# Wide layers as seven products of quarters instead of eight, with sums of weights formed on chip

## The chip, the cores and the metric

One core of one Trainium2 chip runs the whole kernel in one launch. The metric is the time of that launch on the device, in microseconds (us), lower is better. Engines are named as in the profile: PE is TensorE (PEld its weight loads), DVE is VectorE, ACT is ScalarE, POOL is GpSimd, SP is SyncE, which here only issues DMAs. SBUF is the on-chip memory that all engines read; PSUM holds the results of matmuls, in eight banks of 128 x 512 floats.

## The reference

A sequence of 4 x 1024 tokens with 256 channels passes a feed-forward network, a state-space mixing layer, and the same feed-forward network again.

```python
def ffn(x, w1_w, w1_s, w2_w, w2_s, h1_w, h1_s, h2_w, h2_s, w3_w, w3_s):
    lin = lambda x, w, s: einsum("bsi,oi->bso", x, w) * s      # w is ternary: -1, 0 or 1
    h = silu(lin(x, w1_w, w1_s)) * lin(x, w2_w, w2_s)          # 256 -> 1024
    h = gelu(lin(h, h1_w, h1_s))                               # 1024 -> 1024, exact gelu
    h = gelu(lin(h, h2_w, h2_s))                               # 1024 -> 1024
    return lin(h, w3_w, w3_s)                                  # 1024 -> 256

def mixing(x, ...):            # state-space layer: a long convolution over the sequence
    K = s4d_kernel(...)        # 256 channels x 1024 taps
    y = irfft(rfft(x, n=2048) * rfft(K, n=2048))[:1024]
    return gelu(y) @ W.T + b

x = x + 0.5 * ffn(layernorm(x))       # x: [4, 1024, 256] float32
x = x + mixing(layernorm(x))
x = x + 0.5 * ffn(layernorm(x))
```

The two layers `h1` and `h2`, 1024 to 1024, are the wide layers. They hold most of the arithmetic.

## The kernel before

**Tiles and blocks.** The 4096 tokens are cut in blocks of 512. Eight blocks, f0 to f7, go through the first feed-forward network, and eight, g0 to g7, through the second. Tokens lie along the free dimension, 512 to a tile, and channels along the 128 partitions. A block passes through four stages in `ffn`: the gate stage (eight pairs of tiles `pa` and `pb`, 8 matmuls to a pair, silu on ACT at L362 and the product on DVE at L363), the two wide layers (tiles `p`, gelu on ACT at L377), and the last stage (tiles `po`, in `last_squares`, or in `last_tokens` for the block that ends the kernel).

**Two parts.** The matmuls run in the fp32r format, in which a general float32 value is not held exactly. The weights, being -1, 0 or 1, are. An activation is therefore carried in two parts: the high part is a cast on ACT (L367 and L379), the low part is the difference between the value and its cast, a subtraction of two SBUF tiles on DVE (`low_part`, L287). `linear` (L344) multiplies each weight tile with both parts into one PSUM bank. A tile of a wide layer is 8 input chunks x 2 parts = 16 matmuls, 128 x 128 weights by 512 columns, so a layer is 128 of them and the two layers 256. All weights stay in SBUF (`h1_sb` and `h2_sb` take 32 KB a partition each); POOL's DMA queue brings them at the start.

**Mixing layer.** The convolution is done with discrete Fourier transforms as matmuls, and with products and sums of spectra on DVE. This work, `all_aside`, is a generator that is cut in small steps. Between two tiles of a wide layer `ffn` calls `tick()`, which advances it until work worth `STEP_WORK` = 2500 units (130 an operation plus its columns) has been issued, or until it reports a pause, and `ahead()`, which advances the preparation of the next block (load, layer norm, transposition of 32 x 32 squares with a pass through DRAM). Where the mixing layer has nothing to do, `tick()` runs `weight_checks`, which reads all weights again and compares them with the copies in fp32r; if one differed, a second version of the whole would run in float32. The mixing of a sequence starts once both of its blocks have left the first network (f1 for the first sequence), and must be done before its first block in the second one is prepared.

**Order.** Each engine executes its own instructions in a fixed order, made from the order of the calls in the source by a scheduler. The DMAs of SP and those of POOL form two queues. A tile of the pools `half` (19 buffers of 2 KB a partition), `ring` (15, for the two-part activations) or `psum` (8 banks, shared by everything) waits until the last reader of the buffer that it reuses is done. The output additions `y` of a block are on POOL (L406), with the stores issued by POOL (L408).

Of the kernel before, what the change touches and what calls it, by code (L numbers as in the profile page):

```python
# [31 lines left out]
JQ = J // 2  # L32
N_WARM = 9


STEP_WORK, OP_WORK, MIN_WORK = 2500, 130, 300
PAUSE = "pause"
N_CHECKS = 44

# [58 lines left out]
def macaron_layers(  # L98
# [22 lines left out]

    nc = tc.nc
# [7 lines left out]
    psum = ctx.enter_context(tc.tile_pool(name="psum", bufs=8, space=bass.MemoryType.PSUM))  # L130

    work_done = 0
# [16 lines left out]
    def bank(name):  # L149
        return psum.tile([P, 512], F32, tag="ps", name=name)  # L150

    def half(name, *shape, dtype=F32):

        return work.tile([P, *(shape or (512,))], dtype, tag="half", name=name, bufs=19)

    def ring(name, *shape, dtype=F32):

        return work.tile([P, *shape], dtype, tag="ring", name=name, bufs=15)
# [9 lines left out]
    h1_sb = keep.tile([P, KH, HID], wide, name="h1_sb")  # L168
    h2_sb = keep.tile([P, KH, HID], wide, name="h2_sb")
# [12 lines left out]
    k_hat = dram.tile([2 + len(PAIRS), 2, P, 2, D], F32, name="k_hat")  # L182

# [37 lines left out]


# [21 lines left out]
    for t, src in ((h1_sb, h1), (h2_sb, h2)):  # L244
        for k in range(0, KH, 2):
            weights_from.dma_start(t[:, k : k + 2, :], rows(src)[:, k : k + 2, :])
# [38 lines left out]
    def low_part(t, src):  # L285

        return nc.vector.tensor_tensor(t[:, 1, :], src, t[:, 0, :].bitcast(F32), ALU.subtract)  # L287

    def transposed(xn, name):


        pts = [bank(f"pt_{name}_{k}") for k in range(DC)]
# [59 lines left out]
    def ffn(xt, src, dst, blk, name, tick, ahead, final):  # L352


        ha = []
        for m in range(KH):
            pa, pb = bank(f"pa_{name}_{m}"), bank(f"pb_{name}_{m}")
            linear(pa, w1_sb, m, xt)
            linear(pb, w2_sb, m, xt)
            g = half(f"g_{name}_{m}")  # L360
            t = ring(f"ha_{name}_{m}", parts, TB, dtype=wide)
            nc.scalar.activation(g, pa, AF.Silu, scale=sc_sb[:, 0, m : m + 1])  # L362
            nc.vector.scalar_tensor_tensor(  # L363
                g if split else t[:, 0, :], pb, sc_sb[:, 1, m : m + 1], g, ALU.mult, ALU.mult
            )
            if split:
                nc.scalar.copy(t[:, 0, :], g)  # L367
                low_part(t, g)
            ha.append(t)
        for layer, w in ((2, h1_sb), (3, h2_sb)):  # L370
            hb = []
            for m in range(KH):
                ps = bank(f"p{layer}_{name}_{m}")
                linear(ps, w, m, ha)
                t = ring(f"h{layer}_{name}_{m}", parts, TB, dtype=wide)
                g = half(f"g{layer}_{name}_{m}") if split else t[:, 0, :]
                nc.scalar.activation(g, ps, AF.Gelu, scale=sc_sb[:, layer, m : m + 1])  # L377
                if split:
                    nc.scalar.copy(t[:, 0, :], g)  # L379
                    low_part(t, g)  # L380
                hb.append(t)
                ahead()
                if layer == 2 or m < KH - 1:
                    tick()
            ha = hb
        ahead(last=True)
        if name == "f0":
            nc.scalar.mul(w3s_half, w3s_half, 0.5)
        (last_tokens if final else last_squares)(ha, src, dst, blk, name)

    def last_squares(ha, src, dst, blk, name):
# [8 lines left out]
        for k in range(DC):  # L400
            ps = bank(f"po_{name}_{k}")
            linear(ps, w3_sb, k, ha)
# [7 lines left out]
    def last_tokens(ha, src, dst, blk, name):  # L410

        rest = []
        for i in range(0, JT, 2):
            xr = half(f"xr_{name}_{i}", 2, D)
            nc.sync.dma_start(xr, tokens(src, blk, i, 2))
            rest.append(xr)

        def result(ps, i, n):

            for e in range(n):  # L420
                for k in range(KH):
                    for part in range(parts):
                        nc.tensor.matmul(  # L423
                            ps[:, e * D : (e + 1) * D],
                            ha[k][:, part, (i + e) * P : (i + e + 1) * P],
# [16 lines left out]

        y = half(f"y_{name}_0", 2, D)
        ps = bank(f"po_{name}_0")
        result(ps, 0, 2)
        finish(ps, y, rest[0], 0, 2, nc.gpsimd)
        y = half(f"y_{name}_2", 2, D)
        for e in range(2):
            ps = bank(f"po_{name}_{2 + e}")
            result(ps, 2 + e, 1)  # L450
            finish(
                ps[:, 0:D], y[:, e : e + 1, :], rest[1][:, e : e + 1, :], 2 + e, 1, nc.vector
            )

    def weight_checks():

        todo = []
        for src, held in ((w1, w1_sb), (w2, w2_sb), (h1, h1_sb), (h2, h2_sb), (w3, w3_sb)):
            n_k, width = held.shape[1], held.shape[2]
            by = max(1, 512 // width)  # L460
            for k in range(0, n_k, by):
                for c in range(0, width, 512):
                    cols = slice(c, min(c + 512, width))
                    todo.append((rows(src)[:, k : k + by, cols], held[:, k : k + by, cols]))
        assert len(todo) == N_CHECKS

        def load(n):
            given = half(f"given_{n}", *todo[n][1].shape[1:])
# [5 lines left out]
        for n, (src, held) in enumerate(todo):  # L474
            given = following
            if n + 1 < len(todo):
                following = load(n + 1)
            stt(
                given,
                given,  # L480
                0.0,
                held.bitcast(F32),
                ALU.add,
                ALU.not_equal,
                accum_out=miss[:, n : n + 1],
            )
            yield

# [3 lines left out]
        nc.vector.tensor_reduce(total, miss[:, 0:N_CHECKS], axis=mybir.AxisListType.X, op=ALU.add)  # L492
        yield
        ps = psum.tile([1, 1], F32, tag="ps", name="p_bad")
# [109 lines left out]
    def kernel_steps():  # L604
# [7 lines left out]
        for g0 in range(0, DD, group):  # L612
# [34 lines left out]
            def products(d1, a):  # L647
# [3 lines left out]
                if at == 0:  # L651
                    pk = psum.tile([P, per_tile, 2, NB], F32, tag="ps", name=f"pk_{g0 + d1}")
# [46 lines left out]
    def spectrum(rows_of, name, over=1):  # L699
# [22 lines left out]
        def products(q, m):  # L722
            ps = []
            for e in range(2):
                ps.append(psum.tile([P, 2, D], F32, tag="ps", name=f"pf_{name}_{q}_{e}"))
# [17 lines left out]
        for n in (0, 2):  # L743
            qs = order[n : n + 2]
            if n == 0:
                for q, m in zip(qs, ms):
                    products(q, m)
                ms = [matrix(q) for q in order[2:4]]
                yield PAUSE
            for q in qs:  # L750
                sums(q)
            if n == 0:
                for q, m in zip(order[2:4], ms):
                    products(q, m)
            s, t = (u[q] for q in qs)
            halves.append((add(s, t, ALU.add, f"s{n}"), add(s, t, ALU.subtract, f"d{n}")))
            yield PAUSE if n == 0 else None
# [49 lines left out]
    def mix(b, xn):  # L807
# [92 lines left out]
        banks = [[bank(f"pi_{b}_{dc}_{e}") for e in range(2)] for dc in range(DC)]  # L900
        for q, m in enumerate(matrices):
            for e in range(2):
                for dc in range(DC):
                    for part in range(2):
                        nc.tensor.matmul(  # L905
                            banks[dc][e][:, q * P : (q + 1) * P],
# [5 lines left out]
        yts = [[half(f"yt_{b}_{dc}_{e}") for e in range(2)] for dc in range(DC)]  # L912
        for e in range(2):
            for dc in range(DC):
                nc.scalar.activation(yts[dc][e], banks[dc][e], AF.Gelu)
# [38 lines left out]
    done = []  # L954
# [52 lines left out]
    def tick():  # L1007

        nonlocal ticks, allowed, work_done
        ticks += 1  # L1010
        allowed = min(allowed, work_done) + STEP_WORK
        while work_done < allowed:
            at = work_done
            if next(aside, PAUSE) is PAUSE:
                if len(done) > 8 and allowed - work_done > OP_WORK + TB:
# [6 lines left out]
    warm = bank("warm")  # L1022
# [99 lines left out]
```

## Time and profile before

The three runs took 1405.35, 1405.5 and 1405.73 us: a median of 1405.5. The profiled execution took 1405.23 us in all, of which the profile's span is 1403.3 us. TensorE's granted clock was 0.999 over it. Shares are of the span; a group's mean is that of one instruction.

| what | busy or mean | count |
|---|---|---|
| matmuls of wide layers, start of one to start of the next | 226.6 ns | 4096 |
| weight loads (PEld) | 1161.4 us, 83% | 6492 |
| low parts (DVE, L287, 128x512) | 690 ns | 256 in wide layers |
| gelu (ACT, L377, 128x512) | 689 ns | 256 |
| casts (ACT, L379) | 619 ns | 256 |
| ACT table loads (L377) | 1283 ns | 51 |
| gate product (DVE, L363, one operand in PSUM) | 749 ns | 128 |
| additions on POOL (L406, 128x512) | 1.30 us | 30 |
| DMA traffic | 101.27 MB, mean 72 GB/s | |

The busy times of TensorE and of the other engines, and the chain of waits, are shown in the prediction. A duration in a group is how long one instruction took, its own start-up included, and dense instructions of one engine overlap a little. For matmuls the spacing of starts is the figure that adds up to time, since they are pipelined.

### The profile page before, as it was taken

What the parts mean: (1) busy time and instruction counts of PE and PEld (TensorE: products, weight loads), DVE (VectorE), ACT (ScalarE), POOL (GpSimd) and SP (SyncE); (2) the same over time, 40 slices, a digit from 0 to 9 for tenths busy, and PEclk for the clock granted to TensorE, in tenths of its full rate; (3) what the DMA queues carried; (4) which work ended last, traced back from release to release, by engine and by line L of the source; (5) the groups of instructions that cost most, each with busy time, mean ns of one, the idle gap of its engine ahead of it and who ended that gap; (6) DMA issues with size and microseconds to landing.
All of it is one profiled execution on the core that took longest, in us unless ns stands there. A gap on an engine that the chain in (4) does not pass through costs nothing.

```text
span 1403.3 us, 17882 instructions
## 1 busy us (share of the span) xinstructions
PE 1393.0 (99%) x6492; PEld 1161.4 (83%) x6492; DVE 838.6 (60%) x1614; ACT 707.6 (50%) x1070; POOL 266.3 (19%) x398
## 2 busy tenths in 40 slices
PE   8999999999999999999999999999999999999998
PEld 7888888888888888888888888888888888888887
DVE  6896567755547774387773568753566762542412
ACT  5986579644546344354352454533545342553532
POOL 4321012211312120320113201213112121121200
PEclk9999999999999999999999999999999999999999
DMA  9410101112231322422213404132223122511000
GB/s 355 117 20 26 35 16 46 30 48 77 67 96 30 113 71 73 136 60 84 61 53 113 113 31 138 20 97 74 86 70 82 43 63 98 135 22 39 15 16 19
DMA packets 111139, 101.27 MB, mean 72 GB/s; under 512 B 72304, under 2 KB 82544, under 8 KB 111040
## 3 DMA queue, kind: packets, MB, share of 16 engines
q1 hardware_dynamic: 93248, 55.37, 14.6%
q0 software_dynamic: 17520, 44.39, 11.1%
q8 instruction: 53, 0.87, 0.3%
q14 instruction: 46, 0.38, 0.1%
q10 hardware_dynamic: 272, 0.26, 0.1%
HBM read 76.91 MB, written 23.07 MB: 71 GB/s over the span
## 4 chain that ended last, share of the span: by engine, by line
PE 99%; DMA 1%; POOL 0%; DVE 0%; issue 0%; POOLq 0%
PE p_f L344 33%; PE p_g L344 33%; PE po_f L344 4%; PE pa_g L344 4%; PE pb_g L344 4%; PE pa_f L344 4%; PE pb_f L344 4%; PE po_g L344 4%; PE pi L905 2%; PE pf_m L727 2%; PE pw L930 2%; PE pk L654 1%; PE po_g L423 1%; DMA w_sb<-in_w_dram 1%; PE pf_k L727 0%; POOL w_sb L238 0%
## 5 line engine op out<-in xcount | busy, mean ns | idle before, releaser
L287 DVE TENSOR_TENSOR h_g<-g_g,h_g 128x512 fp32r<-128x512 f32 x128 | 88.6, 692 | 249.6 <-ACT h_g L379 249.3
L344 PE MATMUL p_f<-h_f,h_sb 128*128 128x512 f32 x1024 | 237.1, 391 | 0.0
L344 PE MATMUL p_g<-ha_g,h_sb 128*128 128x512 f32 x1024 | 236.2, 390 | 0.0
L344 PE MATMUL p_f<-ha_f,h_sb 128*128 128x512 f32 x1024 | 235.3, 390 | 0.0
L344 PE MATMUL p_g<-h_g,h_sb 128*128 128x512 f32 x1024 | 235.2, 390 | 0.0
L377 ACT ACTIVATE g_g<-p_g,sc_sb 128x512 f32<-128x512 f32 x128 | 88.2, 689 | 278.9 <-PE p_g L344 276.5
L344 PEld LDWEIGHTS p_g<-ha_g,h_sb 128*128 128x128 f32 x1024 | 192.1, 188 | 39.8
L344 PEld LDWEIGHTS p_g<-h_g,h_sb 128*128 128x128 f32 x1024 | 192.1, 188 | 39.8
L344 PEld LDWEIGHTS p_f<-h_f,h_sb 128*128 128x128 f32 x1024 | 191.8, 188 | 40.1 <-DVE h_f L287 0.3
L344 PEld LDWEIGHTS p_f<-ha_f,h_sb 128*128 128x128 f32 x1024 | 191.9, 188 | 39.8
L377 ACT ACTIVATE g_f<-p_f,sc_sb 128x512 f32<-128x512 f32 x128 | 87.7, 689 | 190.0 <-PE p_f L344 189.6
L287 DVE TENSOR_TENSOR h_f<-g_f,h_f 128x512 fp32r<-128x512 f32 x128 | 87.8, 690 | 149.0 <-ACT h_f L379 148.5
L317 POOL DMA_DIRECT2D moved<-sq_g x64 | 34.9, 552 | 330.3 <-DVE sq_g L140 290.7
L379 ACT CAST h_g<-g_g 128x512 fp32r<-128x512 f32 x128 | 79.3, 620 | 4.0
L379 ACT CAST h_f<-g_f 128x512 fp32r<-128x512 f32 x128 | 78.3, 618 | 2.9
L377 ACT ACT_TABLE_LOAD x51 | 65.4, 1283 | 26.0 <-PE p_f L344 14.3
L344 PE MATMUL pa_f<-xt_f,w_sb 128*128 128x512 f32 x256 | 69.0, 390 | 1.1 <-DVE xt_f L299 0.7
L344 PE MATMUL pb_f<-xt_f,w_sb 128*128 128x512 f32 x256 | 68.8, 389 | 0.0
L344 PE MATMUL pa_g<-xt_g,w_sb 128*128 128x512 f32 x256 | 68.4, 389 | 0.0
L344 PE MATMUL pb_g<-xt_g,w_sb 128*128 128x512 f32 x256 | 68.4, 389 | 0.0
L363 DVE SCALAR_TENSOR_TENSOR g_g<-pb_g,sc_sb,g_g 128x512 f32<-128x512 f32 x64 | 47.9, 749 | 31.5 <-PE pb_g L344 19.7
L317 POOL DMA_DIRECT2D moved<-sq_f x56 | 30.8, 556 | 181.2 <-DVE sq_f L140 181.2
(234 smaller groups left out, 1844.4 us busy)
## 6 DMA issues: line engine op xcount, KB each, us to landing
h_sb<-in_h_dram POOLq DMA_DIRECT2D x8, 1024.0 KB, 15.0
given<-in_h_dram SPq DMA_DIRECT2D x32, 256.0 KB, 3.6
kr<-k_hat SPq DMA_DIRECT2D x20, 256.0 KB, 2.6
ki<-k_hat SPq DMA_DIRECT2D x20, 256.0 KB, 2.8
xr_f<-in_x_dram SPq DMA_DIRECT2D x64, 64.0 KB, 2.4
x<-y_f POOLq DMA_DIRECT2D x64, 64.0 KB, 2.2
xm<-x SPq DMA_DIRECT2D x8, 512.0 KB, 3.7
m_m<-in_cosm_dram SPq DMA_DIRECT2D x16, 256.0 KB, 5.2
```

Source lines behind the costliest of these rows:

```text
L287: return nc.vector.tensor_tensor(t[:, 1, :], src, t[:, 0, :].bitcast(F32), ALU.subtract)
L317: stores.dma_start(moved[k].rearrange("(c r) a q -> a r c q", r=SQ)[a], sq[a * SQ : (a + 1) * SQ].rearrange("r c j s -> r c (j s)"),)
L344: nc.tensor.matmul(ps, w[:, k, m * P : (m + 1) * P], acts[k][:, part, :], start=(k == 0 and part == 0), stop=(k == n - 1 and part == parts ...
L363: nc.vector.scalar_tensor_tensor(g if split else t[:, 0, :], pb, sc_sb[:, 1, m : m + 1], g, ALU.mult, ALU.mult)
L377: nc.scalar.activation(g, ps, AF.Gelu, scale=sc_sb[:, layer, m : m + 1])
L379: nc.scalar.copy(t[:, 0, :], g)
L423: nc.tensor.matmul(ps[:, e * D : (e + 1) * D], ha[k][:, part, (i + e) * P : (i + e + 1) * P], w3_sb[:, k, :], start=(k == 0 and part == 0) ...
L654: nc.tensor.matmul(pk[0:NA, at + i, :, :].rearrange("p h b -> p (h b)"), a[:, i].rearrange("p a b -> p (a b)"), qd[d1 // per_tile][:, at + ...
L727: nc.tensor.matmul(ps[e][:, part, :], m[:, e, part, :], rows_of(q + JQ * e), start=True, stop=True)
L905: nc.tensor.matmul(banks[dc][e][:, q * P : (q + 1) * P], vs[q + JQ * e][:, part, dc * P : (dc + 1) * P], m[:, e, part, :], start=(part == ...
L930: nc.tensor.matmul(ps[:, e * D : (e + 1) * D], yts[dc][j // JQ][:, (j % JQ + e) * P : (j % JQ + e + 1) * P], wt_sb[:, dc, :], start=(dc == 0),
```

## The change

A wide layer is Y = A B with A the 1024 x 1024 weights and B the 1024 x 512 activations. Cut both in quarters: A11, A12, A21, A22 of 512 x 512, and B11, B12, B21, B22 of 512 inputs by 256 tokens. Multiplied plainly that is eight products. Winograd's form of Strassen's scheme needs seven:

- weights: S1 = A21 + A22, S2 = S1 - A11, S3 = A11 - A21, S4 = A12 - S2. These are small whole numbers.
- activations: T1 = B12 - B11, T2 = B22 - T1, T3 = B22 - B12, T4 = T2 - B21.
- products: A11 B11, S1 T1, S2 T2, A12 B21, S3 T3, S4 B22 and -A22 T4, with sums between them, some in PSUM by accumulation in the same bank, and three by a copy to SBUF and an addition.

The new function `winograd` writes the seven out in this order. One product is 4 output tiles x 4 input chunks x 2 parts = 32 matmuls of 256 columns. The differences T are formed on POOL (`less`), cast and split as before (`operand`; the low parts of B21 and B22 on POOL, the others on DVE), the intermediate products are copied by ACT (`kept`) and added by DVE (`plus`), and gelu works on pieces of 256 columns (`activated`). Block f0 uses `quartered`, eight products of quarters. Its ticks also run `weight_sums`, which loads the weights in pieces, forms the sums on DVE, ACT and POOL and stores them in DRAM, in `quarters`. From f1 on each product loads its weights, 1 MB, from there into one of four buffers (`slot`), three products ahead, through SP's queue. `h1_sb` and `h2_sb` are gone.

The eight banks of PSUM become six for the feed-forward network and two for the rest. There are fourteen ticks to a layer in place of eight, with `STEP_WORK` 1340. The checks of h1 and h2 no longer compare with copies in SBUF but test whether each weight is -1, 0 or 1, with two DVE operations for one piece in place of one, and begin when f4 is done. The last stage works on one half of the tokens after the other. The spectrum and the inverse transform are put in an order that needs two banks at a time. The core of the diff:

```diff
+QT = TB // 2          # 256 tokens
+QK = KH // 2          # 4 chunks of 128 inputs
+QW = HID // 2         # 512 outputs
+A11, S1, A12, S2, S3, S4, MINUS_A22 = range(7)
+ORDER = (A11, S1, S2, A12, S3, S4, MINUS_A22)
-STEP_WORK = 2500
+STEP_WORK = 1340
...
-    psum = ctx.enter_context(tc.tile_pool(name="psum", bufs=8, ...))
+    def bank(name):
+        return psum.tile([P, 512], F32, tag="ps", name=name, bufs=2)
+    def ffn_bank(i, name):
+        return psum.tile([P, 512], F32, tag=f"ffn{i % 6}", name=name)
+    # half: bufs 19 -> 16, ring: 15 -> 12; piece(name, tag): [P, TB] F32, bufs=6
...
+        quarters = [[dram.tile([P, QK, QW], F32) for i in range(7)] for n in range(2)]
+        h2_raw = dram.tile([HID, HID], F32, name="h2_raw")
...
-    for t, src in ((h1_sb, h1), (h2_sb, h2)):
-        for k in range(0, KH, 2):
-            weights_from.dma_start(t[:, k : k + 2, :], rows(src)[:, k : k + 2, :])
+        for m in range(2):
+            for k in range(2):
+                t = work.tile([P, QK, QW], F32R, tag="slot", bufs=4)
+                weights_from.dma_start(t, quarter_of(h1, m, k))
+                slots.append(t)
+        nc.sync.dma_start(h2_raw, h2)
+        for n, src in enumerate((h1, h2)):
+            nc.sync.dma_start(quarters[n][A11], quarter_of(src, 0, 0))
+            nc.sync.dma_start(quarters[n][A12], quarter_of(src, 0, 1))
...
     def ffn(...):
+        raw = [raw_tile(f"g_{name}_{p}") for p in range(KH // 2)]
...                                    # gate stage writes g into raw, without cast and low part
+        for layer in (2, 3):
+            some = 16 if name == "f0" else 14
+            def step():
+                at += 1
+                if at * KH // some > (at - 1) * KH // some:
+                    ahead()
+                if layer == 2 or at < some:
+                    tick()
+            raw = (quartered if name == "f0" else winograd)(raw, layer, name, step)
+        for k, n in ((0, 0), (1, 1), (0, 1), (1, 0)):
+            held[k, n] = operand(block(raw, k, n), f"hl_{name}_{k}{n}")
+    def operand(quarter, name, by=nc.vector):
+        for p, src in enumerate(quarter):
+            t = ring(f"{name}_{p}", parts, TB, dtype=wide)
+            nc.scalar.copy(t[:, 0, :], src)
+            low_part(t, src, by)
+    def less(a, b, name):
+        out = [piece(f"{name}_{p}", "diff") for p in range(2)]
+        for o, x_, y_ in zip(out, a, b):
+            nc.gpsimd.tensor_tensor(o, x_, y_, ALU.subtract)
+    def product(banks, weights, ops, step, first=True):
+        for p, ps in enumerate(banks):
+            for e in range(2):
+                m = 2 * p + e
+                for c in range(QK):
+                    for part in range(parts):
+                        nc.tensor.matmul(ps[:, e * QT : (e + 1) * QT],
+                            weights[:, c, m * P : (m + 1) * P],
+                            ops[c // 2][:, part, c % 2 * QT : (c % 2 + 1) * QT], ...)
+            step()
+    def quartered(raw, layer, name, step):
+        b = {(k, n): operand(block(raw, k, n), ...) for k, n in ((0, 0), (0, 1), (1, 0), (1, 1))}
+        for m in range(2):
+            for k in range(2):
+                weights = slots.pop(0)
+                for n in range(2):
+                    product(banks[n], weights, b[k, n], step, first=k == 0)
+                load_slot()
+            for n in range(2):
+                activated(out, m, n, banks[n], layer)
+    def winograd(raw, layer, name, step):
+        def times(banks, ops, first):
+            product(banks, slots.pop(0), ops, step, first)
+            load_slot()
+        def plus(sums, banks):
+            for o, ps in zip(sums, banks):
+                nc.vector.tensor_tensor(o, ps, o, ALU.add)
+        b11 = operand(of(0, 0), named("b11"))
+        t1 = less(of(0, 1), of(0, 0), named("t1"))
+        t1_ops = operand(t1, named("t1s"))
+        times(pa, b11, True)
+        p1 = kept(pa, named("p1"))                 # ACT copies of two banks
+        t2 = less(of(1, 1), t1, named("t2"))
+        t2_ops = operand(t2, named("t2s"))
+        times(pd, t1_ops, True)
+        p5 = kept(pd, named("p5"))
+        b21 = operand(of(1, 0), named("b21"), nc.gpsimd)
+        times(pa, t2_ops, False)
+        u2 = kept(pa, named("u2"))
+        t3 = less(of(1, 1), of(0, 1), named("t3"))
+        t3_ops = operand(t3, named("t3s"))
+        times(pe, b21, True)
+        activated(out, 0, 0, plus(p1, pe), layer)  # four gelu of 256 columns
+        b22 = operand(of(1, 1), named("b22"), nc.gpsimd)
+        times(pa, t3_ops, False)
+        activated(out, 1, 1, plus(p5, pa), layer)
+        t4 = less(t2, of(1, 0), named("t4"))
+        t4_ops = operand(t4, named("t4s"))
+        times(pd, b22, False)
+        activated(out, 0, 1, plus(u2, pd), layer)
+        times(pa, t4_ops, False)
+        activated(out, 1, 0, pa, layer)
+    def load_slot():                   # the next quarter: of h2_raw in f0, then quarters[layer][i]
+        t = work.tile([P, QK, QW], F32R, tag="slot", name=name, bufs=4)
+        nc.sync.dma_start(t.bitcast(F32), src)
+        slots.append(t)
+    def weight_sums():                 # one step of it at each tick
+        for layer, src in enumerate((h1, h2)):
+            for c in range(QK):
+                for m in range(2):
+                    for k in range(2):
+                        a[m, k] = piece(..., "diff")
+                        nc.sync.dma_start(a[m, k], quarter_of(src, m, k)[:, c, :])
+                yield
+                nc.vector.tensor_tensor(s1, a[1, 0], a[1, 1], ALU.add)
+                nc.scalar.mul(a[1, 1], a[1, 1], -1.0)
+                nc.gpsimd.tensor_tensor(s2, s1, a[0, 0], ALU.subtract)
+                nc.vector.tensor_tensor(a[1, 0], a[0, 0], a[1, 0], ALU.subtract)
+                nc.gpsimd.tensor_tensor(s4, a[0, 1], s2, ALU.subtract)
+                yield
+                for i, t in ((S1, s1), (S2, s2), (S3, a[1, 0]), (S4, s4), (MINUS_A22, a[1, 1])):
+                    stores.dma_start(quarters[layer][i][:, c, :], t)
+                yield
...
     def last_squares(act, src, dst, blk, name):
-            linear(ps, w3_sb, k, ha)
+        for n in (1, 0):               # token halves: 64 matmuls of 256 columns in place of 32 of 512
+            for o, ps in enumerate(banks):
+                ...
```

## The prediction

> **What bounds the kernel now.** I read the page from the top: busy time, the chain that ended last, then the groups.
>
> ```profile
> PE 1393.0 (99%) x6492; PEld 1161.4 (83%) x6492; DVE 838.6 (60%) x1614; ACT 707.6 (50%) x1070; POOL 266.3 (19%) x398
> ...
> PEclk9999999999999999999999999999999999999999
> ...
> PE 99%; DMA 1%; POOL 0%; DVE 0%; issue 0%; POOLq 0%
> ```
>
> TensorE (PE) is 99% of the span and of the chain, at full clock; its waits add up to 4 us, all before 11 us. Only its work, or a new wait, can move the time. What one matmul costs is read from the chain in order of time (start, us, engine, tile, count):
>
> ```profile
> 455.25 58.03 PE p_f L344 x256
> ...
> 549.54 7.14 PE pi L905 x64
> ...
> 1388.99 7.94 PE po_g L423 x64
> ```
>
> The wide layers of one block are 256 matmuls of 512 columns in 58.03 us: 226.7 ns each, 226.6 over many blocks. The 64 matmuls of 256 columns take 7.94 us, of which 0.2 us is a wait for DVE: 121 ns. So half the columns cost 53%, not 50%. The 128-column row (111.6 ns) says that a new weight tile can follow about every 112 ns, so at 256 columns the weight load doesn't yet rule.
>
> How full are the others inside the wide layers (windows from the first p tile to the first po tile; busy PE, PEld, DVE, ACT, POOL, clock, DMA share, GB/s)?
>
> ```profile
> 455.07:513.11 58.04, 58.04 (x258) 48.05 (x256) 47.88 (x90) 24.77 (x36) 5.47 (x10) 1.00 0.32 96
> 809.63:874.63 65.00, 65.00 (x290) 54.12 (x288) 48.05 (x99) 30.02 (x43) 5.49 (x10) 1.00 0.28 87
> ```
>
> DVE reaches 82% there, 11 us for this block's low parts and the rest the interleaved work of the mixing layer ("aside"); POOL is nearly idle. Last, the timeline where a POOL addition meets DVE, twice:
>
> ```profile
> 626.64 1.30 POOL L406 TENSOR_TENSOR y_f<-xr_f,y_f 128x512 f32<-128x512 f32 x1
> ...
> 626.80 1.71 DVE L287 TENSOR_TENSOR ha_f<-g_f,ha_f 128x512 fp32r<-128x512 f32 x1
> ...
> 1145.29 1.31 POOL L406 TENSOR_TENSOR y_g<-xr_g,y_g 128x512 f32<-128x512 f32 x1
> ...
> 1146.17 0.75 DVE L363 SCALAR_TENSOR_TENSOR g_g<-pb_g,sc_sb,g_g 128x512 f32<-128x512 f32 x1 [0.23 <-PE pb_g L344]
> ```
>
> The low part takes 0.69 us elsewhere; begun 0.16 us into a POOL operation it takes 1.71 and ends 0.57 us after POOL does. The second DVE operation, which reads one operand from PSUM, is not touched.
>
> **What the Trainium skill says.** "SBUF — State Buffer", Who interferes with whom: VectorE and GpSimd share one port; a VectorE operation with two SBUF inputs, or in a two-port mode, and a GpSimd operation that reads SBUF exclude each other for a whole instruction. The trace agrees (1.71 us against 0.69). "TensorE: Matmul & The Clock Gate", Back-to-back issue gap: columns/2.4 + 2.5 ns, 215.8 and 109 ns here; measured 226.6 and 121, which I use. "DMA: Bandwidth & Descriptors", Queues, rings and completion order: each queue has its own ring on each DMA engine, worked in ring order, and an engine takes turns between queues; no run here shows two full queues. Same page, Where 436 GB/s comes from: that is the ceiling; the trace moves 416 to 422 GB/s in the windows from 10 to 30 us.
>
> **The change, part by part** (counts from the built instruction streams, durations from the rows).
>
> *TensorE.* Out go 4576 matmuls of 512 columns (16 x 256 wide, 15 x 32 in `last_squares`): 4576 x 0.2266 = 1036.9 us. In come 8192 of 256 columns (15 x 448, 512 for f0 in quarters without Strassen, 15 x 64): 8192 x 0.121 = 991.2. **-45.7 us**, not an eighth of the 928 us of wide layers, since the fixed part of a matmul is paid twice as often. Ends: 0.1200 (226.6 ns less 256 columns at 2.4 GHz) gives -54, 0.124 (the wait left in) -21. All of it is on the path.
>
> *Start.* SP now carries, ahead of all else but x and constants, `h2_raw` (4.19 MB) and four quarter copies (4.19 MB), DRAM to DRAM, then the first pieces for the sums (1.05 MB), while POOL's queue brings w1, w2 and h1. DVE's built order has the first sum (`s1` of chunk 0) ahead of the gating product of the fifth of eight tiles, and its operands are last in SP's ring. Behind it wait the gating products and the low parts of the first operands; with six banks, three pairs, PE stops at the eighth tile. Best case: 9.7 MB from SP and the 3.5 MB that PE needs, at 420 GB/s, 31.5 us, + 2 to start, + 4 for the DVE work behind: first wide layer at 37.5 instead of 24.2, 13 us late. With the two queues sharing equally SP's 9.7 MB need 46 us: 26 us late. I take 18; nothing PE now waits for is taken away, so no gain. Block f0 also ends its quarters without a later product as cover: gelu, cast, low part, +2. **+20 us.** The rest of the sums (8 x 4 loads, 8 x 5 stores, 16 POOL and 16 DVE operations) lies in f0's 62 us of wide layers; f0 and f1 move some 30 MB in the 80 us after that, 375 of 420 GB/s, little margin.
>
> *The port.* Per Strassen block POOL gets 24 operations (8 `less`, 4 low parts, in each layer) beside its 2 `y` additions: 26 x 1.30 = 33.8 us in which no two-input DVE operation can run. DVE: a layer's 8 low parts become 10 and 6 additions from PSUM, so +177 us in all, + 22 for second operations in the checks; 838.6 becomes about 1037. I summed, by the built order between the first gate tiles of successive blocks, the DVE work that needs the port (0.63 us per two-input 128x512, the spacing of dense ones), POOL's, and PE's time:
>
> | block | PE | DVE on port | + POOL | excess |
> |---|---|---|---|---|
> | f0 | 83.3 | 65.4 | 86.2 | 2.9 |
> | f2 | 76.5 | 48.4 | 82.2 | 5.7 |
> | f5 | 77.5 | 56.2 | 90.0 | 12.5 |
> | f7 | 76.5 | 52.2 | 86.0 | 9.5 |
> | g1 | 76.3 | 55.1 | 88.9 | 12.6 |
> | g3 | 80.1 | 47.9 | 81.7 | 1.6 |
>
> The other ten stay under PE. **+45 us**: there PE waits for operands. Ends: 0 if it is hidden, 70 if gate and last stage can't take their share.
>
> *Chains.* In a layer POOL does t1, t2, t3, t4 and b21 in order: b21's second half comes last, ready 10.8 us after the gate's end at 1.3 us an operation, wanted at 12.2 (product 4). Each wait for the port (up to 0.6 us) uses that up; so do four 0.55 us store issues in layer 3. After product 7 the last operand needs 2 gelu, cast, low part, twice, about 5 us, and PE's cover is 5.3. I put 1 us on each of some 20 layers outside the table: **+20**, ends 0 and 60.
>
> *At nothing.* ACT: +640 gelu halves less 376 whole, +360 casts, about +260 us, to some 970: two thirds of the span; without that cover a table load, 1.28 us, would go straight into the chain above. Weight loads: 1.05 MB per product, 271 GB/s during 3.87 us, four buffers, so three products (11.6 us) of lead for some 3 us; the other traffic (27 to 139 GB/s in these windows) fits below 420. On SP the k_hat, matrix and xr loads now stand behind loads that wait for a product's end; their users come a product later. The 2-bank pool for aside matmuls and 16 instead of 19 `half` buffers: the next tile waits for ACT and DVE, counted in the chains.
>
> **Sum** against the profiled execution (span 1403.3 us, run 1405.2; the median, 1405.5, is 0.3 above): 1405.2 - 45.7 + 20 + 45 + 20 = **1444 us**.
>
> **Rivals.** (1) *Faster: the port is hidden.* The place is f5, f7 and g1; the price is the 45 us and most of the chain waits. It decides from the point where a POOL operation holds the port under 0.82 us of its 1.30 (f5: 56.2 + 26 x 0.82 = 77.5), or POOL's operations fall beside PSUM reads. For it: such reads are not delayed. Against: four overlaps in the trace all last to POOL's end. Then 1405.2 - 45.7 + 20 + 12 = 1391. (2) *Weights late.* Below about 215 GB/s for them (10 loads in the 49 us from the first product to the last) every further 10% costs 5 us a block: at 195, 75 us, 1520 in all. Against: 420 measured, one big load under way at a time. (3) *Seven cost as much as eight.* At 126.6 ns a matmul the gain is nil: 1490. Against: the row at 121 has the same tile sizes. (4) *Only the start is worse than thought*, sign open: within the ranges above.
>
> **How the numbers follow.** The port bounds: 0.56, 1444, from 1412 (half the port, few chain waits) to 1500. Port hidden: 0.31, 1370 to 1402, and half of its worse start ends near nothing. Weights late 0.06, seven as eight 0.03, rest 0.04. No change that a measurement could tell is 0.2%, 2.8 us. Faster 0.31, same 0.06, slower 0.63. Range 1382 to 1500; the likeliest case alone 1412 to 1495.
>
> **What would show it.** Right: 256-column matmuls 120 to 122 ns apart where nothing waits; PE idle some 15 us before the first wide layer, behind the first sum; PE idle in f5, f7, g1 behind low parts; DVE low parts averaging above 0.8 us; POOL operations back to back. Wrong: low parts at 0.69 us and PE above 97% (rival 1), or PE waiting for `q` loads (rival 2), or 127 ns spacing (rival 3).

## The result: 1690 us, a fifth slower, and the profile after

The changed kernel takes 1690.4 us (median of four runs, 1685.8 to 1695.7) against 1405.6 us for the kernel before on the same chip: a ratio of 1.2026, 95% interval 1.1978 to 1.2074. The forecast was 1444 us with a range of 1382 to 1500. The sign was right, the size was not. The profiled execution took 1695.65 us, its span is 1693.9 us, the mean granted clock 0.92.

The page after, busy time and then the granted clock in 40 slices:

```profile
PE 1453.4 (86%) x10108; PEld 1368.3 (81%) x10108; DVE 1332.6 (79%) x1903; ACT 906.4 (54%) x1673; POOL 861.2 (51%) x810
...
PEclk7897989897999979999999998899998899979999
```

Two numbers are not what the sum made them. TensorE's busy time rose by 60 us where the sum had 46 less, at a clock that is full throughout in only 9 of the 40 slices, and it sits idle for 240 us. DVE is busy for 1333 us where about 1037 were estimated, with just the operations that were counted. So its operations became longer. Which ones, the groups by form tell (line, engine, operation, out<-in, shapes, count, busy us and mean ns, idle before):

```profile
L329 DVE TENSOR_TENSOR t2s_g<-t_g,t2s_g 128x512 fp32r<-128x512 f32 x32 | 57.2, 1806 | 6.4 <-ACT t2s_g L479 5.1
...
L329 DVE TENSOR_TENSOR hl_g<-h_g,hl_g 128x512 fp32r<-128x512 f32 x64 | 43.1, 685 | 13.6 <-ACT hl_g L479 13.4
...
L571 DVE TENSOR_TENSOR p_g<-p2a_g,p_g 128x512 f32<-128x512 f32 x16 | 11.0, 688 | 5.6 <-PE p2a_g L498 5.4
```

One and the same subtraction takes 1.81 us on T2, formed while POOL works through its list, and 0.685 us at the end of a block, when POOL has done. The addition that reads one operand from PSUM (L571) is at 0.68 to 0.69 us in every group. The timeline of g0's first wide layer shows how it comes about, DVE, POOL and PE in turn (start, us, engine, line, operation, count, idle before and its releaser):

```profile
906.50 1.76 DVE L150 TENSOR_TENSOR v_True<-u_i,w_i 128x512 f32<-128x512 f32 x1
908.18 1.75 DVE L150 SCALAR_TENSOR_TENSOR v_False<-w_i,u_i 128x512 f32<-128x512 f32 x1
909.86 1.75 DVE L150 SCALAR_TENSOR_TENSOR v_True<-w_i,u_i 128x512 f32<-128x512 f32 x1
911.52 3.43 DVE L329 TENSOR_TENSOR t2s_g<-t_g,t2s_g 128x512 fp32r<-128x512 f32 x2
```

```profile
904.29 3.42 POOL L488 TENSOR_TENSOR t_g<-g_g,g_g 128x512 f32<-128x512 f32 x2
907.67 3.38 POOL L488 TENSOR_TENSOR t_g<-t_g,g_g 128x512 f32<-128x512 f32 x2
911.02 3.38 POOL L329 TENSOR_TENSOR b_g<-g_g,b_g 128x512 fp32r<-128x512 f32 x2
```

```profile
906.56 0.28 PE L498 MATMUL p2a_g<-t2s_g,w 128*128 128x256 f32 x1
913.32 1.22 PE L498 MATMUL p2a_g<-t2s_g,w 128*128 128x256 f32 x4 [6.48 <-DVE t2s_g L329]
915.01 4.58 PE L498 MATMUL p2a_g<-t2s_g,w 128*128 128x256 f32 x27 [0.46 <-DVE t2s_g L329]
```

DVE and POOL take turns, one operation each: DVE starts one every 1.68 us, POOL one every 1.69. DVE executes in order, so five operations of the mixing layer (the last three are shown) stand ahead of T2's low part and pass at this pace. PE waits 6.48 us. More is lost behind the wait: the last row's 27 matmuls take 4.58 us, where 27 at 120 ns take 3.24. The granted clock was 0.50 from 910.7 us, inside the wait, to 917.5.

That the scheme is sound where DVE has nothing else to do shows in the windows of the last block, g7, beside f0 (from the first wide tile to the first tile of the last stage; columns as in the prediction):

```profile
51.19:135.28 84.09, 65.72 (x513) 65.11 (x511) 68.30 (x118) 52.14 (x85) 49.77 (x69) 0.91 0.92 305
...
1624.26:1679.71 55.45, 54.27 (x450) 53.86 (x448) 34.68 (x36) 38.24 (x75) 32.57 (x21) 1.00 0.54 190
```

g7's wide layers take 55.45 us, against 58.03 before. T2's low parts are stretched there too, to 1.62 us, but no other work stands ahead of them on DVE. f0's take 84.1 instead of 58.2, and begin at 51.2 us instead of 24.2.

### The profile page after: what moved, and what is told of

It is laid out like the page before. It is cut to its first block, busy times and chain, and to the rows that moved or that the text cites. A ratio compares the mean times of both kernels' runs of the same rounds, so it can differ in the third digit from the quotient of the medians.

```text
span 1693.9 us, 27029 instructions
## 1 busy us (share of the span) xinstructions
PE 1453.4 (86%) x10108; PEld 1368.3 (81%) x10108; DVE 1332.6 (79%) x1903; ACT 906.4 (54%) x1673; POOL 861.2 (51%) x810
## 5 line engine op out<-in xcount | busy, mean ns | idle before, releaser
L525 ACT ACTIVATE h_g<-p_g,sc_sb 128x256 f32<-128x256 f32 x128 | 58.1, 502 | 85.1 <-DVE p_g L571 84.9
L525 ACT ACTIVATE h_f<-p_f,sc_sb 128x256 f32<-128x256 f32 x144 | 63.0, 496 | 71.1 <-DVE p_f L571 70.8
L664 PE MATMUL po_f<-hl_f,w_sb 128*128 128x256 f32 x512 | 74.2, 305 | 29.9 <-ACT hl_f L479 16.0
L664 PEld LDWEIGHTS po_f<-hl_f,w_sb 128*128 128x128 f32 x512 | 69.7, 210 | 34.0 <-ACT hl_f L479 17.4
L386 PEld LDWEIGHTS pb_f<-xt_f,w_sb 128*128 128x128 f32 x256 | 49.4, 196 | 36.4 <-DVE g_f L416 15.7
L498 PE MATMUL p_f<-b_f,w_f 128*128 128x256 f32 x512 | 65.7, 293 | 7.3 <-ACT h_f L525 7.3
L498 PEld LDWEIGHTS p_f<-b_f,w_f 128*128 128x128 f32 x512 | 65.4, 202 | 7.9 <-ACT h_f L525 7.7
L664 PE MATMUL po_g<-hl_g,w_sb 128*128 128x256 f32 x448 | 59.1, 294 | 6.4 <-DVE hl_g L329 6.4
L664 PEld LDWEIGHTS po_g<-hl_g,w_sb 128*128 128x128 f32 x448 | 57.6, 201 | 7.1 <-DVE hl_g L329 6.8
L386 PEld LDWEIGHTS pa_f<-xt_f,w_sb 128*128 128x128 f32 x256 | 48.7, 193 | 18.2 <-issue 4.0
```

The source lines that it names most:

```text
L386: nc.tensor.matmul(ps, w[:, k, m * P : (m + 1) * P], acts[k][:, part, :], start=(k == 0 and part == 0), stop=(k == n - 1 and part == parts ...
L498: nc.tensor.matmul(ps[:, e * QT : (e + 1) * QT], weights[:, c, m * P : (m + 1) * P], ops[c // 2][:, part, c % 2 * QT : (c % 2 + 1) * QT], ...
L525: nc.scalar.activation(raw[2 * k + p][:, n, c, :], src[:, c * QT : (c + 1) * QT], AF.Gelu, scale=sc_sb[:, layer, m : m + 1],)
L664: nc.tensor.matmul(ps[:, n * QT : (n + 1) * QT], w3_sb[:, k, o * P : (o + 1) * P], act(k, part, n * QT, (n + 1) * QT), start=(k == order[0 ...
```

## The experiments

### POOL's operations: moved, unhooked, taken away

**e1_dve**: all arithmetic of a Strassen layer on DVE.

```diff
-            nc.gpsimd.tensor_tensor(o, x_, y_, ALU.subtract)      # less
+            nc.vector.tensor_tensor(o, x_, y_, ALU.subtract)
-        b21 = operand(of(1, 0), named("b21"), nc.gpsimd)          # b22 likewise
+        b21 = operand(of(1, 0), named("b21"))
```

> The changed kernel (1690 us) with the eight differences `less` and the four low parts of B21 and B22 of each Strassen layer on DVE in place of POOL. Port theory (a two-input DVE operation and a POOL operation that read SBUF take turns, so that each costs about 1.7 us while both queues are full): DVE two-input operations go back to 0.65 to 0.7 us, DVE busy falls from 1332.6 to about 1270 us although it has 360 operations more (838.6 + 177 + 22 + 360 x 0.65), and the time falls to 1430 to 1520. Chain theory (POOL is merely slow, 1.3 us an operation in a chain that PE waits for): the time falls about as much, but the durations of the DVE operations that stay are what they were. Load theory (DVE has too much to do and has its aside work ahead of the operands): DVE now has more, so 1690 or above.

Measured: 1486.1 us, ratio 1.0575 (1.0558 to 1.0593). DVE has 360 operations more and is busy 79 us less. The page, and the same group as above:

```profile
PE 1380.2 (93%) x10108; PEld 1311.8 (88%) x10108; DVE 1253.9 (85%) x2263; ACT 916.9 (62%) x1682; POOL 310.9 (21%) x450
```

```profile
L329 DVE TENSOR_TENSOR t2s_g<-t_g,t2s_g 128x512 fp32r<-128x512 f32 x32 | 21.4, 681 | 0.1
```

T2's low part fell from 1806 to 681 ns. The load theory is out; the chain theory predicts no such fall.

**e2_loose** and **e3_silent**: POOL works, but nobody waits for it; then it doesn't work at all.

```diff
-        t1_ops = operand(t1, named("t1s"))                        # t2, t3, t4 likewise
+        t1_ops = operand(of(0, 1), named("t1s"))
-        b21 = operand(of(1, 0), named("b21"), nc.gpsimd)          # b22 likewise
+        b21 = high_only(of(1, 0), named("b21"))                   # cast; POOL's result is not read
```

> The changed kernel with POOL's differences and low parts still issued at the same places, but nobody waits for them: the operands for T1 to T4 are split from the quarters B12, B22, B12 and B21 themselves, and the products of B21 and B22 use the high part twice (POOL writes that low part to a tile that nobody reads). PE, ACT and DVE have the same operations as before this edit; the products are those of other operands. Port theory: DVE's low parts are still stretched well above 1 us while POOL runs, PE still waits for them, 1560 to 1690 us. Chain theory: POOL is off the path, so about what the kernel without POOL's operations takes, 1420 to 1450.

> As the kernel e2_loose, with POOL's differences and low parts left out altogether. Port theory: DVE low parts at 0.69 us, and a time of PE's work (about 1360 us with the ends) + 27 us of late start + some waits: 1400 to 1450. Chain theory: the same as e2_loose. Load theory: PE still waits for low parts behind aside work, above 1550.

Measured: 1666.1 us and 1441.6 us, one run each. The pages, e2_loose first:

```profile
PE 1432.0 (86%) x10108; PEld 1351.9 (81%) x10108; DVE 1366.8 (82%) x1903; ACT 898.7 (54%) x1674; POOL 853.3 (51%) x810
```

```profile
PE 1362.7 (95%) x10108; PEld 1300.8 (90%) x10108; DVE 1038.6 (72%) x1903; ACT 902.7 (63%) x1674; POOL 310.1 (22%) x450
```

The low parts that stand in T2's place, of one of the two layers, e2_loose first:

```profile
L329 DVE TENSOR_TENSOR t2s_g<-h_g,t2s_g 128x512 fp32r<-128x512 f32 x16 | 23.0, 1450 | 0.6 <-ACT t2s_g L479 0.6
```

```profile
L329 DVE TENSOR_TENSOR t2s_g<-h_g,t2s_g 128x512 fp32r<-128x512 f32 x16 | 11.9, 758 | 1.7 <-ACT t2s_g L479 1.7
```

This pair decides it. PE, DVE and ACT have the same numbers of instructions in both, and nobody reads what POOL's extra work makes. Its presence costs 224 us and makes DVE's 1903 operations 328 us longer. One way to wait for POOL is left in e2_loose, for a buffer that POOL still reads; its trace has one such wait that e3_silent's has not, 2.1 us on ACT. With POOL silent DVE is busy 1038.6 us, the 1037 of the estimate. The change itself is at 1690, 24 us above e2_loose; that this is the wait for POOL's results is likely, but no run shows it alone.

**e4_pool_in_before** and **e7_memset_in_before**: the suspected cost put alone into the kernel before.

```diff
                     low_part(t, g)
+                    for _ in range(2 - m % 2):                    # e4
+                        nc.gpsimd.tensor_tensor(g, g, t[:, 0, :].bitcast(F32), ALU.subtract)
+                    for _ in range(4 - 2 * (m % 2)):              # e7
+                        nc.gpsimd.memset(g, 0.0)
```

> The kernel before, with 24 POOL subtractions of 128x512 a block added in its wide layers (two after each even tile, one after each odd one; they overwrite a value that has been used for the last time, so nobody waits for the result). Port theory: DVE busy rises from 838.6 by 100 to 250 us as operations that meet POOL take 1 to 1.75 us, ACT and PE durations stay, and most of it is covered since DVE has the room: 1405 to 1470 us. Chain and load theories: DVE's durations and the time stay, 1405.5.

> As e4_pool_in_before (1519 us), with two POOL memsets of 128x512 in place of each POOL subtraction: about the same POOL time (48 x 0.6 us a block), at the same places, on the same tiles, but POOL reads nothing. If what DVE waits for is POOL's reading of SBUF, DVE's low parts stay at 0.69 us and the time at 1405 to 1410. If any work of POOL holds DVE up (access to SBUF as such), it is 1500 to 1520 again.

Measured: 1519.1 us, ratio 1.0809 (1.0791 to 1.0827), and 1412.1 us (one run). The pages, e4 then e7:

```profile
PE 1436.6 (95%) x6492; PEld 1181.4 (78%) x6492; DVE 1083.4 (71%) x1614; ACT 710.3 (47%) x1072; POOL 827.5 (55%) x782
```

```profile
PE 1395.3 (99%) x6492; PEld 1161.2 (82%) x6492; DVE 860.3 (61%) x1614; ACT 708.6 (50%) x1071; POOL 665.4 (47%) x1166
```

POOL subtractions make DVE's time 245 us longer, as foretold; POOL memsets, which read nothing, 22 us, and the time is 2 us above what was expected for that case. The memsets came out shorter in all than the subtractions (399 us of added POOL time against 561), but the kind of DVE operation tells the two apart: `tensor_tensor` of 128x512 floats, most of them with two SBUF inputs, takes 683 ns on average before, 684 in e7 and 998 in e4. So what these operations share with POOL is a path for reading SBUF. The Trainium skill says the same ("SBUF — State Buffer", Who interferes with whom: a DVE instruction with two SBUF inputs contends with a POOL instruction that reads SBUF, not with one that only writes it). The port theory erred in one thing: it took DVE's room for cover and allowed 65 us, and 113 came. Where the cover fails can be read in e4's timeline of PE, and what a gap costs in the windows after it (us, busy PE, PEld, DVE, ACT, POOL, clock, DMA share, GB/s):

```profile
92.63 2.65 PE L344 MATMUL po_f<-h_f,w_sb 128*128 128x512 f32 x11
97.39 6.70 PE L344 MATMUL po_f<-h_f,w_sb 128*128 128x512 f32 x21 [2.10 <-DVE h_f L287]
```

```profile
96.00:97.40 1.40, 0.01 (x1) 0.01 (x1) 1.40 (x4) 1.38 (x4) 0.00 (x0) 1.00 0.02 6
...
98.40:99.40 1.00, 1.00 (x4) 0.77 (x3) 1.00 (x3) 0.03 (x2) 0.41 (x1) 0.50 0.00 0
99.40:100.40 1.00, 1.00 (x4) 0.81 (x3) 1.00 (x5) 1.00 (x2) 0.00 (x0) 0.50 0.00 0
...
101.40:102.40 1.00, 1.00 (x6) 0.75 (x5) 1.00 (x3) 0.90 (x3) 1.00 (x1) 1.00 0.00 0
```

A wait of 2.1 us for a low part, then 3.4 us at half clock: 21 matmuls take 6.70 us instead of 4.76. In e4 PE is idle for 80 us of the span, and its busy time is 44 us above that of the kernel before with the same matmuls; the stretches at half clock hold 70 us of busy PE, half of which, 35, is most of the 44.

### The first two blocks

**e8_gated_dve**, **e9_gated_change**: copies and sums kept out of the way of the first loads, on e1_dve and on the change.

```diff
-        nc.sync.dma_start(h2_raw, h2)                             # and the four quarter copies
+            if split and name == "f0" and m == KH - 2:
+                with tc.issue_after(silu.ins):
+                    nc.scalar.dma_start(h2_raw, h2)
-                        nc.sync.dma_start(a[m, k], quarter_of(src, m, k)[:, c, :])
+                        with tc.issue_after(loads[0].ins):
+                            nc.sync.dma_start(a[m, k], quarter_of(src, m, k)[:, c, :])
```

> As e1_dve (1486 us), with the copies in DRAM issued by ACT behind the silu of the seventh of eight gate tiles of f0, and the loads for the sums issued behind the first load of a slot, so that neither is in the DMA rings while w1, w2 and h1 come in, and DVE's first sum stands behind all gating products. In e5_late_sums and h_all_whole the copies were moved in the program, but had nothing to wait for and still ran at the start: w1 and w2 landed at 32 us instead of 8, and the first wide layer began at 51 to 52 us in all of them. If the copies' traffic is what delays it (start theory), it now begins at 24 to 28 us and the time is 25 to 35 us less: 1450 to 1462. If it is the form of the loads of h1 (four squares in place of eight strips), it stays at 51 us and 1486.

> The same gating of copies and sums on the changed kernel itself (1690 us), POOL's share of the Strassen layers as it is. Start theory: 25 to 40 us less, 1650 to 1665. The rest of the loss, about 250 us, is left, since it belongs to DVE and POOL.

Measured: 1485.2 us (ratio 1.0563, 1.0548 to 1.0579) and 1693.8 us (1.2037, 1.2020 to 1.2054). Nothing was won on either. In e8 the first wide layer did begin at 24.8 us, but f2's gate began at 245.0 us; in e1_dve at 239.7, before at 176.1.

**e11_pool_copies** and **e12_no_sums**: the copies and the sums' loads at the end of POOL's queue; then the sums left out.

```diff
+            nc.gpsimd.dma_start(h2_raw, h2)                       # behind the last load of weights
-                        nc.sync.dma_start(a[m, k], quarter_of(src, m, k)[:, c, :])
+                        nc.gpsimd.dma_start(a[m, k], quarter_of(src, m, k)[:, c, :])
-        next(sums_of_weights, None)                               # e12: no sums
-                    yield quarters[layer][i], f"w_{n}_{layer}_{i}", layer
+                    yield quarter_of(h2_raw, i // 2 % 2, i % 2), f"w_{n}_{layer}_{i}", None
```

> As e1_dve (1486 us) with the copies and the loads for the sums moved from SP's queue to the end of POOL's, behind all loads that f0 needs, the first sum three ticks later, and the sign change on DVE in place of ACT. In e8_gated_dve the first wide layer did begin at 24.8 us (from 51.1), but ACT then stood 19 us at the issue of its fifth copy, with a silu behind it, and gelu and casts waited behind the sums' loads later, so f1's gate began at 158 us and nothing was won. If the order of transfers is the whole of f0's loss (start theory), f1's gate begins at 100 to 115 us in place of 150 and the time is 1437 to 1455 us. If the traffic itself is (8.4 MB read and written for copies, 8.4 MB read and 10.5 MB written for sums, in 60 us), f1's gate begins at 130 or later and the time is above 1465.

> As e11_pool_copies (1490 us), with the sums of weights and their copies left out: every Strassen product loads a quarter of h2 itself, 1 MB from the same copy in DRAM (the products are of other weights). All loads of slots stay, and DVE, ACT and POOL have the same work but for the sums. In e1, e8 and e11 the delay sat at the first wide layer, at f0's ticks, or at f0's end, but f2's gate began at 240, 245 and 242 us each time, 64 to 69 us after the 176 us of the kernel before. If the chain of sums (eight rounds of load, DVE, POOL, DVE, POOL, store, 12 us each, which f1 cannot begin without) is what is conserved, f2's gate begins at 178 to 190 us and the time is 1425 to 1440 us. If it is the frame (slots, banks, f0 in quarters), it begins at 220 or later, and 1470 or more.

Measured: 1490.6 us (1.0591, 1.0566 to 1.0617) and 1424.8 us (1.0131, 1.0114 to 1.0148). In e11 f0's wide layers ran from 24.0 to 87.5 us, before from 24.2 to 82.5. Then PE waited for DVE. The waits of PE up to 170 us, and of DVE (who waited for whom, us in total, times, longest):

```profile
PE po_f L667 <- DVE hl_f L332: 17.3, 1, 17.3
PE pa_f L389 <- DVE xt_f L379: 10.5, 1, 10.5
```

```profile
DVE s L638 <- DMA a<-in_h_dram: 38.5, 5, 11.7
```

Five times, 38.5 us in all, DVE stands at the first operation of a sum, whose pieces have not come, with low parts and x tiles queued behind. POOL's timeline of e11 gives the pace, the first operation of the eight sums being at

```profile
62.41 1.67 POOL L640 TENSOR_TENSOR s<-s,a 128x512 f32<-128x512 f32 x1 [4.15 <-DVE s L638]
...
88.35 1.26 POOL L640 TENSOR_TENSOR s<-s,a 128x512 f32<-128x512 f32 x1 [1.33 <-DVE s L638]
...
161.74 3.21 POOL L640 TENSOR_TENSOR s<-s,a 128x512 f32<-128x512 f32 x1 [3.94 <-DVE s L638]
```

These are the first, the third and the eighth. Seven rounds in 99 us, 14 us each: load four pieces, DVE, POOL, DVE, POOL, five stores, and the next loads wait for the buffers that the stores hold. The first matmuls of f2's gate, in e11 and e12:

```profile
242.06 1.09 PE L389 MATMUL pa_f<-xt_f,w_sb 128*128 128x512 f32 x4
```

```profile
183.80 1.09 PE L383 MATMUL pa_f<-xt_f,w_sb 128*128 128x512 f32 x4
```

Without the sums 58 us are gone by then, and 66 us of the whole. So the sums, which f1 cannot begin without, are what was conserved while the delay moved from the start to the end of f0. e12 leaves out their chain and their transfers together, so the two are not told apart; in five stretches from 62 to 175 us the DMA engines moved 178 to 343 GB/s in e11, below the 416 to 422 of the kernel before's start, which speaks for the chain; but in one of them, 112 to 125 us, they were busy all the time.

### Versions with some or all blocks in the old form

**e5_late_sums**, **h_all_whole**, **e6_mixed**, **e10_mixed_gated** compute some blocks, or all, in the old form (512 columns) on loaded quarters. e6 and e10 were meant to win.

```diff
+WHOLE = ('f0', 'f1')            # e5; all sixteen in h_all_whole
+WHOLE = ('f0', 'f1', 'f2', 'f5', 'f6', 'f7', 'g1', 'g3')     # e6 and e10
+        if SUMS_AFTER in done and ticks % 2:                      # "ticks % 2" in e10 alone
+            next(sums_of_weights, None)
```

> As e1_dve (1486 us: everything of the Strassen layers on DVE), and f0 and f1 computed as in the kernel before (512 columns, eight output tiles of sixteen matmuls), with their weights in the same four slots; the copies in DRAM are made during f0's wide layers and the sums of weights are formed in f1, so that nothing of them lies ahead of the first matmuls. f2 to g7 are Strassen blocks. In e1_dve f1's gate begins at 132 + 18 = 150 us, 60.5 us later than the 89.7 us of the kernel before; f2's gate begins at 239.7, against 176.1. If the loss of the first two blocks is the sums and copies (start theory), f2's gate begins at 178 to 185 and the whole takes 1421 to 1435 us. If it is the six banks, the slots or the weight loads, it stays above 1460.

> The same frame (slots and weights loaded for every block, six banks and two, 16 `half` buffers, 12 ring buffers), but all sixteen blocks computed as in the kernel before, with no Strassen block and no sums. It prices the frame alone: 1405 to 1412 us if loads, banks and buffers cost next to nothing; 1430 or more if they do.

> As e5_late_sums, with Strassen (all on DVE) only in f3, f4, g0, g2, g4, g5, g6 and g7, where DVE had room in e1_dve, and the 512-column form in the other eight. Eight blocks can gain 58.03 + 7.25 - 53.75 - 7.68 = 3.85 us each, 31 us: 1375 us at best. With waits of 1 to 3 us in some of them, each with its half-clock window: 1380 to 1400, faster than before. If DVE is too full even there, 1405 to 1420.

> As e6_mixed (1447 us; Strassen on DVE in eight of sixteen blocks), with the copies issued by ACT behind f0's first gelu, the sums spread over f1 and f2 at every second tick, their loads behind the loads of slots, and the sign change on DVE in place of ACT. Start theory: first wide layer at 24 to 28 us (-25), its half-clock windows gone (-8), f1 without its 7 to 10 us of waits: 1400 to 1412. A version that beats the kernel before needs 1402 or less.

Measured: e5 1486.8 us (1.0576, 1.0560 to 1.0592), h_all_whole 1451.7 (1.0319, 1.0303 to 1.0335), e6 1447.6 (1.0303, 1.0284 to 1.0322), e10 1423.7 (1.0134, 1.0112 to 1.0156). e6 and e10 missed all that was expected of them; e5 and h_all_whole missed the cheaper of their two cases. One reason is seen in the first three: the copies in DRAM depended on nothing and ran at the start all the same, and the first wide layer began at 51 to 52 us. e10 cured that (24.4 us) and lost 13 us in f0's wide layers all the same; f2's gate began 16 us late. From f2's gate to the end e10 takes 1228 us, and the kernel before 1227: eight Strassen blocks just pay for the frame of loaded slots and fewer buffers, and for the sums that ran on into f2 and f3. h_all_whole shows that frame's price without any Strassen block: from f1's gate to the end 1337 us against 1314; PE's waits that the profile names are 2.1 us or less each. No version here beats the kernel before.

## Why the prediction was wrong

The steps in the order of its sum, with what the runs put in their place:

| step | predicted | measured | from |
|---|---|---|---|
| TensorE's matmuls | -45.7 | -54 | 32 matmuls in 3.84 us in g7: 120.0 ns, the prediction's other end |
| start | +20 | +66 | e11_pool_copies less e12_no_sums |
| port, with the clock behind its waits | +45 | +224 | e2_loose less e3_silent |
| chains | +20 | +24 | the change less e2_loose |
| rest | 0 | +24 | e3_silent, 1441.6, less (1405.6 - 54 + 66) |

The differences come from unlike kernels, so that they add up (1405.6 - 54 + 66 + 224 + 24 + 24 = 1690) is in part by construction; the rest is what e3_silent leaves.

**The port** was the right mechanism with the wrong size, and this is the failing step: the table took DVE's and POOL's demands on the port over a whole block and let the sum exceed PE's time by an excess. That holds if the work may lie anywhere in the block. It may not: most of POOL's twelve operations of a layer lie just behind the gate, the T operands are wanted within the next 10 to 15 us, and in just that stretch DVE's operations on SBUF tiles, the mixing layer's five as well, run at POOL's pace. g4 to g6, which stay under PE's time in the sum, show it too: g5's wide layers take 78.5 us and PE is busy in 62.3 of them. In place of the 45 us came 224: between e3_silent and e2_loose PE's idle time grows by 155 us and its busy time by 69.

**The clock** was not in the sum at all, and it is part of the 224: the stretches at half clock hold 150 us of busy PE in e2_loose and 34 in e3_silent, and half of the difference, 58 us, is most of the 69. Over the traces of the change, e1, e2, e3 and e4, of PE's gaps above 0.1 us with no other within 8 us, those under 1.5 us (42) were never followed by half clock, those of 1.5 to 3 us in 9 of 26, those of 3 us and more in all 19, and half clock then lasted 4.3 us beyond the gap on average. A gap of 4 us so costs about 6 us, an estimate: its length and half of the 4.3. In the change's profile 273 us are at half clock, with 187 us of busy PE. The Trainium skill has this under "TensorE: Matmul & The Clock Gate", Part 1: a free-running window of some 3.4 us, and half clock after an idle one. The prediction drew on that page for the spacing and passed this over. The traces agree on the length of the windows, with stretches at half clock of 3.41, 6.83 and 10.24 us; they add that a gap of little more than half a window can be enough.

**The start** was half seen. The prediction saw the first DVE sum behind the copies (DVE waited 12.3 us for it, PE 9.1 us), and the first wide layer did begin 27 us late, the far end of its 13 to 26. But it costed the remaining sums at nothing, in "f0's 62 us of wide layers". They take about 95 us as a chain, from 47 to 142 us in the change, and f1 waits for its end.

**What held.** Weight loads are not late: PE waited 5.7 us for them (two groups, 4.5 and 1.2). ACT, at 906 us, is no bound. Weight loads of PE keep up with 256 columns. So rivals 2 and 3 are out. Rival 1, the port hidden, is out by e2_loose and e4_pool_in_before. Its number, 1391 us, would have been optimistic even with a silent POOL: e3_silent is at 1441.6, and e12_no_sums, with no sums and POOL's work on DVE, at 1425, DVE busy for 85%.

The gain itself was real where nothing was laid on top of it. From f2's gate to the end e3_silent takes 1201 us, the kernel before 1227 and e12_no_sums 1245 (its profiled execution was 6 us above its median). So the seven products won 26 us there as long as the twelve operations of a layer that POOL had been given were left out, and doing them on DVE cost some 40, more than was won. e3_silent multiplies other operands, so it shows what was to be won and is no version that could be used.

**What stays open.** Whether those 40 us of e12_no_sums are DVE's load or the longer chains through DVE and ACT, and what makes the 23 us of the frame in h_all_whole, loaded slots or smaller pools, was not tried.

## What to carry to other kernels

Fewer matmuls are worth only what the other engines can feed: here an eighth of the products was at best 3.85 us a block, and each block's additions had to fit into an engine that was 82% full already. Before work goes to an idle POOL, lay its operations beside DVE's in the stretch where the results are wanted, not in the average, and count 1.7 us for each DVE operation of 128x512 floats with two SBUF inputs that meets one. And price a wait of PE by its length and the half clock after it.

## What the runs showed of the hardware

- DVE and POOL, both with full queues, alternate operation by operation: 1.68 us a pair of 128x512 operations. Alone, dense ones start 0.60 us apart on DVE and 1.25 on POOL, 1.85 in sum. Neither is starved, both are slowed, DVE the more.
- It isn't only operations with two SBUF inputs, and for the others POOL needn't read. Beside e7's memsets, `tensor_scalar` of 128x512, with one SBUF tensor, goes from 433 to 614 ns on average and casts of that size from 427 to 603; about 19 of e7's 22 us lie in such one-input operations. In e4's DVE timeline two `tensor_scalar` of 128x256 with one SBUF tensor take 0.74 us together, and the next two, beside a POOL subtraction, 1.71:

```profile
87.09 0.74 DVE L140 TENSOR_SCALAR x_f<-x_f,mv_f,rstd_f 128x256 f32<-128x256 f32 x2
...
88.34 1.71 DVE L140 TENSOR_SCALAR x_f<-x_f,mv_f,rstd_f 128x256 f32<-128x256 f32 x2
```

- An issue of a DMA can hold an engine: in e8_gated_dve ACT stood 19 us at the issue of its fifth copy in a row, with a silu behind it.
